# A planned kernel of four transformer layers: feature bias by small products, first layernorm of the mixing as its own steps, new costs in the planner

## The chip, the cores and the metric

The kernel runs on one core of one Trainium2 chip. A core has five engines with an instruction queue each: TensorE (PE: matrix products, with weight loads of its own, PEld), VectorE (DVE), ScalarE (ACT), GpSimd (POOL), and SyncE (SP), which issues transfers. The metric is the time on the device in microseconds (us), lower is better.

## The reference, cut to what matters

The input is one sequence of 2048 tokens with 128 features. Four layers follow one another. Each part begins with a layernorm, and its output is added to the running x:

- L0: attention with 16 heads of 64, then a mixture of 8 experts with a capacity per expert.
- L1: causal attention with 16 heads of 64, then a gated mixing of each token with the one before it.
- L2: an attention that the kernel folds into one 128x128 product, then a feed-forward of 512 with ternary weights.
- L3: attention with 16 heads, a mask by regions and a bias, then a feed-forward of 512 with binary weights.

The two parts that the change touches compute this:

```python
# the mixing (L1's feed-forward), on h = layernorm(x)
x_prev = jnp.concatenate([zeros, h[:, :-1, :]], axis=1)
xr = mu_r * h + (1.0 - mu_r) * x_prev
xk = mu_k * h + (1.0 - mu_k) * x_prev
out = sigmoid(xr @ W_r.T) * (square(relu(xk @ W_k.T)) @ W_v.T)
```

For L3's bias five small networks score each token: a hidden layer of 64 with gelu, then one sigmoid each. The five scores of a token, weighted by a softmax of `faw` per head, give one number per token and head, and this is what the kernel holds in `bias`.

## The kernel before, in words

**Tiling.** x stays in the core's memory as 16 tiles of 128 tokens (`x`), and the layernormed x as its transpose, features on partitions (`xT`, 128 x 2048). Attention runs over 8 pairs of heads, and in each pair over 8 groups of 256 query tokens. A group has 8 strips of 32 queries. A score step (L482) makes the scores of one strip and both heads: keys are cut in four quarters, and each quarter takes 32 partitions of the output, so that queries and key quarters stand on partitions and 512 keys (fewer under the causal mask) on columns. DVE scans each bank for its lowest value while it copies it out of PSUM (L492). The lowest values are turned, reduced and spread (L544, L552, L560, L567). ACT exponentiates (L594). DVE transposes 32x32 blocks (L611). PE weighs the values (L626). The head sums are added and inverted (L645, L657), the output is projected (L671), scaled (L681) and added to x by POOL (L699).

**The order of the work.** It isn't written out by hand. Every piece is a `Step` with a key (a tick, a place and its number), an engine, a cost in us, the steps that it waits for, and the buffers that it takes and uses. `run()` (L119) is a list scheduler: it walks through modelled time, and for each engine takes the step that can start first by key, with `HOP` (0.15) from engine to engine; buffers come free when the users of an older holder have ended. Steps are issued to the engines in this order, and on the chip each engine works its queue off in order, waiting where its input isn't there. The costs only set the order: they are numbers in the code, such as `max(0.25, 0.0019 * n)` for a score step of n columns with 0.1 on top for causal and 0.07 for masked ones (L500), and `0.06 + 0.00436 * self.width(4 * j)` for a transpose (L613).

**Buffers.** `Ring` and `Held` (L78, L86) hand out rotating buffers: `MISC` (three PSUM banks for all small products), `BANKS` (four PSUM banks for scores), `MID` (four), `MIXED` (three) and `PAIRED` (two buffers of 128 x 512).

**Between L1's and L3's attention.** `rest()` (L1063) is called for five spans of tiles, (0,4), (4,4), (8,4), (12,2) and (14,2). It contains the first layernorm (`normalise`, L1089), the copy of the span's last column of xT to one of two columns of `edge` (L1091), which the next span needs as its previous token, and then the mixing: ACT scales the shifted xT (L1070) and the column from `edge` (L1072), DVE adds (L1075), PE multiplies (L1104, L1079, L1083) with relu, square and sigmoid between (L1109, L1114, L1121), DVE and POOL or DVE gate and add (L1128, L1136). Then come the folded attention of L2 (L1087, L1145) and its feed-forward (L955, L964, L977, L988), with a layernorm in front of each and one behind for L3.

`features()` (L1186) makes the bias for a chunk of 512 tokens, four times. Three products and gelus (L1194, L1199), three products to five scores (L1207) and a sigmoid (L1213) give the scores `fs`, 5 x 512. The attention needs the bias with the queries of a strip on all four quarters of the partitions, so POOL copies the scores of four strips four times over (L1221, four times a chunk), PE multiplies these 128 columns by the head weights (L1228), and DVE copies the result into `bias` (L1234). The chunks get ticks around the spans' own: chunk 0 one below span (8,4), chunk 1 one below (12,2), chunks 2 and 3 one and two above (14,2).

In the page's names, a buffer has its ring's name without its number: `t` is MISC, `s` BANKS, `e` ROWS, `mid` any of MID, MIXED and PAIRED, `big` the weights of the feed-forwards.

Of the kernel before, what the change touches and what calls it, by code (L numbers as in the profile page):

```python
# [58 lines left out]
def network(ctx: ExitStack, tc: tile.TileContext, a: dict, out: bass.AP):  # L59
# [18 lines left out]
    class Ring:  # L78


        def __init__(self, pool, name, shape, bufs, ordered=True):
            self.bufs, self.takers, self.held, self.ordered = bufs, [], [], ordered
            self.make = lambda: pool.tile(list(shape), F32, tag=name, name=name, bufs=bufs)
            rings.append(self)

    class Held:  # L86


        def __init__(self, ring):
            self.ring, self.users = ring, []  # L90
# [28 lines left out]
    def run():  # L119
# [18 lines left out]
        for _ in range(len(steps)):  # L138
# [18 lines left out]
            for h in s.takes:  # L157
                h.t = h.ring.make()
                h.ring.held.append(h)
# [74 lines left out]
    def normalise(add, t0, n, after, before=(), row=None, hurry=False):  # L234


        mv, xn, pt = Held(MEANS), Held(NORMED), Held(MISC)
# [128 lines left out]
    class Pair:  # L366
# [19 lines left out]
        def projected(self, add, c, to, which, s, takes):  # L386
            pp, b = Held(MISC), self.layer.biases[which]
# [18 lines left out]
        def valued(self, add, c):  # L406
            pv, v = Held(MISC), self.v[c]
# [13 lines left out]
    class Group:  # L421
# [37 lines left out]
        def score(self, add, add_scan, k):  # L459
# [40 lines left out]
            us = max(0.25, 0.0019 * n) + (0.1 if causal else 0.07 if masked else 0.0)  # L500
# [25 lines left out]
        def spread_lowest(self, add, add_later, j, found):  # L526

            low, shift, pm, pm2 = self.lows[j], self.shifts[j], Held(MISC), Held(MISC)
# [79 lines left out]
        def turn(self, add, j, h, made):  # L608
            def do():
                e = self.e(h)[:, bass.ts(j, 4), 0 : self.width(4 * j)]  # L610
                nc.vector.transpose(e, e)  # L611

            return add(DVE, 0.06 + 0.00436 * self.width(4 * j), do, made, uses=self.rows)  # L613
# [24 lines left out]
        def sum_up(self, add, made):  # L638

            ps, r = Held(MISC), Held(SHARES)  # L640
# [21 lines left out]
        def project_out(self, tick, weighed, r):  # L662

            y, pair, oT = [Held(MISC) for h in range(2)], self.pair, self.oT
# [88 lines left out]
    def output_bias(add):  # L753
        wo, pr = Held(DOUBLE), Held(MISC)
# [27 lines left out]
    def folded(add):  # L782
        q2T, av = [Held(MID) for k in range(4)], Held(MID)
        pb, pa, pt, pw = (Held(MISC) for k in range(4))
# [44 lines left out]
    moe_w = Held(DOUBLE)  # L829
# [4 lines left out]
    def experts(add, t0, after):  # L834

        r, pl, pc, pp, pb, pickT = Held(ROUTES), Held(MISC), Held(MISC), Held(MISC), Held(MISC), Held(PAIRED)
# [71 lines left out]
        for i in range(4):  # L908
            pe, parts = [Held(MISC) for half in range(2)], Held(PAIRED)
# [37 lines left out]
    def feed_forward(add, t0, n, after, full, w1T, b1, func, w2T):  # L947

        hT, made, po = [Held(MID) for f in range(NC)], [], Held(MISC)
        for f in range(0, NC, 2):  # L950
            ph = [Held(MISC) for k in range(2)]
# [43 lines left out]
    edge = keep([P, 2], "edge")  # L995
    rests = [keep([P, 1], n) for n in ("rest_r", "rest_k")]
    ternary_w = Held(DOUBLE)

    def ternary(add):
# [14 lines left out]
        for i in range(2):  # L1014
            tot, g, half, less = (keep([P, 1], f"{n}{i}") for n in ("tot", "g", "half", "less"))
            pg, low = Held(MISC), Held(MID)
# [44 lines left out]
    edges = []  # L1061

    def rest(add, t0, n, after, hurry, made):  # L1063
        m = P * n
        xr, xk, ka, r = Held(MIXED), Held(MIXED), Held(MIXED), Held(PAIRED)
        pk, pr, pv, po = (Held(MISC) for k in range(4))
        xs, own = x[:, t0 : t0 + n, :], len(edges) % 2

        def parts(to, part):
            nc.scalar.mul(to.t[:, 1:m], xT[:, bass.ds(PAD + P * t0, m - 1)], part)  # L1070
            before = edge[:, 1 - own : 2 - own] if t0 else xT[:, PAD - 1 : PAD]
# [13 lines left out]
        def attend():  # L1085
            for i in range(n):
                nc.tensor.matmul(pv2.t[:, bass.ts(i, P)], lhsT=xT[:, cols(t0 + i)], rhs=w2, start=True, stop=True)  # L1087

        done, _ = normalise(add, t0, n, after, L1_read(t0, n), hurry=hurry)  # L1089
        kept = add(  # L1090
            DVE, 0.15, lambda: nc.vector.tensor_copy(edge[:, own : own + 1], xT[:, bass.ds(PAD + P * (t0 + n) - 1, 1)]),  # L1091
            [done] + (edge_read[-1] if edge_read else []),
        )
        read, mixed = [kept], []
        for to, part, mu in ((xk, rests[1], mu_k), (xr, rests[0], mu_r)):
            s = add(ACT, 0.3 + wide(m), lambda to=to, part=part: parts(to, part), [done] + edges[-1:] + made, takes=[to])
            mixed.append(add(DVE, 0.1 + 0.00125 * m, lambda to=to, mu=mu: mix(to, mu), [s], uses=[to]))
            read += [s, mixed[-1]]
        edge_read.append(read[1::2])
        edges.append(kept)  # L1100
# [41 lines left out]
        pv2 = po  # L1142
# [17 lines left out]
    edge_read, bu_added, ob_added = [], [], [[] for c in range(4)]  # L1160

    def L1_read(t0, n):
        return L1.readers[t0 // 4]
# [7 lines left out]
    def feature_weights(add):  # L1171

        pf = Held(MISC)
# [12 lines left out]
    def features(add, c):  # L1186

        hm, made = [Held(MID) for j in range(3)], []
        fs, pf = Held(MIXED), Held(MISC)
        for j in range(3):  # L1190
            n, ph = P if j < 2 else DH, Held(MISC)
# [12 lines left out]
        def score():  # L1204
# [5 lines left out]

        add(PE, 1.85, score, made, takes=[pf, fs], uses=hm)
        scored = add(
            ACT, 2.6, lambda: nc.scalar.activation(fs.t[0:NF, :], pf.t[0:NF, :], AF.Sigmoid, bias=eb2),  # L1213
            uses=[pf, fs],
        )
        for k in range(4):
            some, pbias = Held(PAIRED), Held(MISC)

            def spread(k=k, some=some):
                strips = fs.t[0:NF, :].rearrange("p (g q) -> p g q", q=Q)[:, 4 * k : 4 * k + 4, :]  # L1220
                nc.gpsimd.tensor_copy(  # L1221
                    some.t[0:NF, :].rearrange("p (g c q) -> p g c q", c=4, q=Q),
                    strips.unsqueeze(2).to_broadcast([NF, 4, 4, Q]),
                )

            def weigh(some=some, pbias=pbias):
                for i in range(4):
                    nc.tensor.matmul(  # L1228
                        pbias.t[:, bass.ts(i, H)], lhsT=some.t[0:NF, bass.ts(i, P)], rhs=fwT, start=True, stop=True
                    )  # L1230

            def copy(k=k, pbias=pbias):
# [176 lines left out]
```

## Time and profile before

| what | value |
|---|---|
| runs shown, median of three | 3634.2 us (3632.11 to 3635.78) |
| the profiled execution's own time | 3627.2 us |
| its span, from first to last instruction | 3625.3 us |
| mean granted PE clock | 0.984 |
| busy: PE, DVE, ACT, POOL | 97%, 92%, 72%, 16% |
| scores on PE (L482, f32) | 1514.0 us |
| weighing on PE (L626) | 1302.4 us |
| scans on DVE (L492) | 1658.7 us |
| transposes on DVE (L611) | 1504.6 us |
| exponentials on ACT (L594) | 1969.3 us |

The profile is one execution. A duration in it is that of one instruction; consecutive instructions of one engine may overlap by some tens of ns, so that the time from start to start tells what one costs. A matmul that is held back while it is in the pipeline counts as busy. In the tables, "idle before" tells how long the engine rested ahead of an instruction, and the name behind the arrow what ended that rest. One product in float32 appears as two matmuls and two weight loads ("passes").

### The profile page before, as it was taken

The numbers are of one execution on the slowest core, as the hardware profiler recorded it, in microseconds if no ns is written. First come the engines' busy times: TensorE is split into PE (matmuls) and PEld (weight loads), VectorE is DVE, ScalarE is ACT, GpSimd is POOL, SyncE is SP. The second block draws the span as 40 slices with busy tenths as digits, with TensorE's granted clock in tenths as the row PEclk, the third lists the DMA queues.
The fourth block names the chain that finished last, engine by engine and source line by source line (L and its number), as shares of the span: only waits on it lengthen the run. The fifth ranks groups of instructions, "written<-read, shape, count | busy, mean of one in ns | idle before, by whom it ended". The sixth has DMA issues, their size and how long they took to land. (4 is left out here: it accounts for less than half of the span.)

```text
span 3625.3 us, 112352 instructions
## 1 busy us (share of the span) xinstructions
PE 3522.5 (97%) x46250; PEld 1798.6 (50%) x46250; DVE 3333.3 (92%) x8275; ACT 2611.1 (72%) x7940; POOL 574.6 (16%) x1172
## 2 busy tenths in 40 slices
PE   8999999999999999999999988899999999999998
PEld 3444444444444455655555645445444454444544
DVE  8999999999999979888888874699999999999995
ACT  5677777777777667788888866477776766777775
POOL 1111011101111242111111134111111111111112
PEclk9999999999999999999999998899999999999999
DMA  1000000000000000000000000000000000000000
GB/s 45 2 5 2 5 5 2 5 2 5 5 2 5 1 5 8 6 6 6 6 6 6 6 2 4 4 5 5 2 5 2 5 5 2 5 2 2 2 5 10
DMA packets 22938, 18.77 MB, mean 5 GB/s; under 512 B 3556, under 2 KB 21612, under 8 KB 22426
## 3 DMA queue, kind: packets, MB, share of 16 engines
q1 hardware_dynamic: 22362, 11.55, 1.1%
q8 instruction: 363, 5.95, 0.7%
q14 instruction: 149, 1.22, 0.1%
q0 software_dynamic: 64, 0.06, 0.0%
HBM read 10.60 MB, written 1.05 MB: 3 GB/s over the span
## 5 line engine op out<-in xcount | busy, mean ns | idle before, releaser
L594 ACT ACTIVATE e<-e,shift 128x512 f32<-128x512 f32 (+15 forms) x3072 | 1969.3, 644 | 182.0 <-DVE shift L578 174.9
L492 DVE TENSOR_SCALAR_CACHE_REDUCE e<-s 128x512 f32<-128x512 f32 (+15 forms) x3072 | 1658.7, 588 | 58.1 <-PE s L482 57.0
L482 PE MATMUL s<-kT,qT 64*32 64x512 f32 (+8 forms) x24576 | 1514.0, 534 | 25.5 <-DVE e L492 24.1
L611 DVE STREAM_TRANSPOSE e<-e 128x2048 f32<-128x2048 f32 (+10 forms) x768 | 1504.6, 1961 | 21.9 <-ACT e L594 20.7
L626 PE MATMUL o<-e,v 128*64 128x256 f32 (+1 forms) x10496 | 1302.4, 386 | 13.3 <-DVE e L611 11.9
L626 PEld LDWEIGHTS o<-e,v 128*64 128x64 f32 x10496 | 731.1, 137 | 587.6 <-issue 233.4
L482 PEld LDWEIGHTS s<-kT,qT 64*32 64x32 f32 x24576 | 429.1, 105 | 490.2 <-DVE e L492 239.0
L594 ACT ACTIVATION_READ_ACCUMULATOR e<-e,shift 128x1 f32 x3072 | 580.0, 189 | 0.0
L560 POOL COPY all_low<-all_low 8x128 f32<-8x128 f32 x384 | 108.0, 281 | 1953.3 <-DVE all_low L552 1953.3
L699 POOL TENSOR_TENSOR x<-x,part 128x256 f32<-128x256 f32 x384 | 280.7, 731 | 562.8 <-ACT part L681 547.4
L681 ACT ACTIVATE part<-t,r 128x128 f32<-128x128 f32 x768 | 218.8, 366 | 148.9 <-PE t L671 144.8
L686 ACT COPY oT<-o 128x256 f32<-128x256 f32 x192 | 70.7, 368 | 274.7 <-PE o L626 274.6
L492 DVE DVE_READ_ACCUMULATOR e<-s 128x1 f32 x3072 | 229.7, 75 | 0.0
L390 PE MATMUL t<-xT,w 128*128 128x512 f32 x384 | 204.2, 625 | 2.7 <-ACT xT L277 2.0
L482 PE MATMUL s<-beyond,eye 64*32 64x32 bf16 x2560 | 159.8, 177 | 0.0
L671 PEld LDWEIGHTS t<-w,oT 64*128 64x128 f32 x1536 | 103.9, 188 | 98.3 <-issue 67.2
L671 PE MATMUL t<-w,oT 64*128 64x128 f32 x1536 | 141.4, 299 | 2.8 <-ACT oT L686 1.5
L482 PEld LDWEIGHTS <-regions 64*32 64x32 bf16 x1024 | 74.4, 93 | 130.1 <-issue 105.3
L586 ACT COPY shift<-t 128x8 f32<-128x8 f32 x256 | 42.2, 165 | 131.0 <-PE t L567 131.0
L552 DVE TENSOR_REDUCE all_low<-t 8x32 f32<-8x128 f32 x384 | 100.7, 262 | 27.8 <-PE t L544 26.9
L482 PE MATMUL s<-picks,regions 64*32 64x8 bf16 x1024 | 122.1, 166 | 0.0
L567 PEld LDWEIGHTS t<-ident,all_low 8*128 8x128 f32 x384 | 51.2, 133 | 134.9 <-issue 75.9
(181 smaller groups left out, 1790.8 us busy)
## 6 DMA issues: line engine op xcount, KB each, us to landing
w<-in_L_wq SPq DMA_DIRECT2D x24, 64.0 KB, 1.9
w<-in_L_wk SPq DMA_DIRECT2D x24, 64.0 KB, 2.1
w<-in_L_wv SPq DMA_DIRECT2D x24, 64.0 KB, 2.0
w<-in_L_wo SPq DMA_DIRECT2D x24, 64.0 KB, 2.1
x<-in_x SPq DMA_DIRECT2D x4, 256.0 KB, 4.7
out_x<-x SPq DMA_DIRECT2D x3, 256.0 KB, 2.3
big<-in_L_wo SPq DMA_DIRECT2D x1, 512.0 KB
big<-in_moe_w SPq DMA_DIRECT2D x1, 512.0 KB
```

Of the source, the lines that this page charges most:

```text
L390: nc.tensor.matmul(pp.t, lhsT=self.w.t[:, which, :], rhs=xT[:, cols(4 * c, 4)], start=True, stop=True)
L482: nc.tensor.matmul(s[h].t[on, bass.ds(first, size)], lhsT=lhsT, rhs=rhs, start=m == 0, stop=m == len(terms) - 1,)
L492: nc.vector.tensor_scalar(self.e(h)[:, i, 0:n], s.t[:, 0:n], 1.0, None, ALU.mult, ALU.min, accum_out=self.lows[j].t[:, h, i % 4 : i % 4 + 1],)
L552: lambda: nc.vector.tensor_reduce(all_low.t, pm.t[0:NS, 0:P].rearrange("p (c q) -> p q c", q=Q), AX.X, ALU.min),
L560: lambda: nc.gpsimd.tensor_copy(all_low4.t, all_low.t.unsqueeze(1).to_broadcast([NS, 4, Q])),
L594: nc.scalar.activation(e, e, AF.Exp, bias=self.shifts[j].t[:, h, i % 4 : i % 4 + 1], scale=-1.0, accum_out=self.sums.t[:, h, i : i + 1],)
L611: nc.vector.transpose(e, e)
L626: nc.tensor.matmul(self.o.t[bass.ds(DH * h, DH), first(t) : NS, :], lhsT=self.pair.v[c].t[:, t % 4, bass.ds(DH * h, DH)], rhs=self.e(h)[:, ...
L671: nc.tensor.matmul(y[h].t[:, bass.ts(j, P)], lhsT=oT.t[half, bass.ts(j, P)], rhs=pair.w.t[half, 3, :], start=True, stop=True,)
L681: nc.scalar.mul(part.t[:, j, :], y[h].t[:, bass.ts(j, P)], r.t[:, j, h : h + 1])
L686: lambda: nc.scalar.copy(oT.t, self.o.t.rearrange("p i q -> p (i q)")),
L699: POOL, 0.74, lambda part=part: nc.gpsimd.tensor_tensor(xs, xs, part.t, ALU.add), [divided], uses=[part]
```

## The change

There are four edits. First, buffers get names of their own for the profile. Second, two costs of the planner change: a score step from 0.0019 to 0.002 per column, its causal extra from 0.1 to 0.14 and its masked extra from 0.07 to 0.05, and a transpose from 0.06 + 0.00436 per column to 0.05 + 0.0042. Third, the first layernorm of the mixing and the copy of its last column become `first_norm`, called for all spans ahead of `rest`, with the same ticks; `edge` has a column for every tile, so that the copy doesn't wait until the column of two spans ago has been read. Fourth, the feature bias: PE multiplies 128 tokens at a time by the head weights (`weigh`, 4 products instead of 16), ACT copies the 128 x 64 results (`some`), 16 products with columns of the identity hand them to the four quarters of partitions (`hand_out`), and one DVE copy puts them into `bias`.

```diff
-            us = max(0.25, 0.0019 * n) + (0.1 if causal else 0.07 if masked else 0.0)
+            us = max(0.25, 0.002 * n) + (0.14 if causal else 0.05 if masked else 0.0)
...
-            return add(DVE, 0.06 + 0.00436 * self.width(4 * j), do, made, uses=self.rows)
+            return add(DVE, 0.05 + 0.0042 * self.width(4 * j), do, made, uses=self.rows)
...
-    edge = keep([P, 2], "edge")
+    edge = keep([P, NT], "edge")
...
+    def first_norm(add, t0, n, after, hurry):
+        done, _ = normalise(add, t0, n, after, L1.readers[t0 // 4], hurry=hurry)
+        last = t0 + n - 1
+        to, some = edge[:, last : last + 1], xT[:, bass.ds(PAD + P * (t0 + n) - 1, 1)]
+        kept[t0 + n] = add(DVE, 0.15, lambda: nc.vector.tensor_copy(to, some), [done])
+        return done
...
-        done, _ = normalise(add, t0, n, after, L1_read(t0, n), hurry=hurry)
-        kept = add(
-            DVE, 0.15, lambda: nc.vector.tensor_copy(edge[:, own : own + 1], xT[:, bass.ds(PAD + P * (t0 + n) - 1, 1)]),
-            [done] + (edge_read[-1] if edge_read else []),
-        )
-        read, mixed = [kept], []
+        read, mixed = [kept[t0 + n]], []
+        needs = [done] + made + ([kept[t0]] if t0 else [])
...
+        def weigh():
+            for i in range(4):
+                nc.tensor.matmul(
+                    pbias.t[:, bass.ts(i, H)], lhsT=fs.t[0:NF, bass.ts(i, P)], rhs=fwT, start=True, stop=True
+                )
+
+        def hand_out():
+            for q in range(4):
+                for i in range(4):
+                    nc.tensor.matmul(
+                        pall.t[bass.ts(q, Q), bass.ts(i, 4 * H)],
+                        lhsT=ident[:, bass.ts(i, Q)],
+                        rhs=some.t[:, 0 : 4 * H],
+                        start=True,
+                        stop=True,
+                    )
+
+        def copy():
+            to = bias[:, bass.ts(c, 16), :].rearrange("p (t i) h -> p i t h", i=4)
+            nc.vector.tensor_copy(to, pall.t[:, 0 : 16 * H].rearrange("p (i t h) -> p i t h", i=4, h=H))
...
-            made = add(POOL, 0.6, spread, [scored], takes=[some], uses=[fs])
-            add(PE, 0.8, weigh, [made, fwT_made], takes=[pbias], uses=[some])
-            L3.biased[c].append(add(DVE, 0.16, copy, uses=[pbias]))
+        add(PE, 0.6, weigh, [scored, fwT_made], takes=[pbias, some], uses=[fs])
+        made = add(ACT, 0.25, lambda: nc.scalar.copy(some.t[:, 0 : 4 * H], pbias.t[:, 0 : 4 * H]), uses=[pbias, some])
+        add(PE, 1.2, hand_out, [made], takes=[pall], uses=[some])
+        L3.biased[c].append(add(DVE, 0.4, copy, uses=[pall]))
...
-    for t0, n in spans:
-        rest(planner(L1.left(t0, n)), t0, n, L1.outputs(t0, n) + [bu_added[t0 // 4]], n < 4, made)
+    done = {}
+    for t0, n in mix_spans:
+        done[t0] = first_norm(
+            planner(L1.left(t0, n)), t0, n, L1.outputs(t0, n) + [bu_added[t0 // 4]], n < 4
+        )
+    for t0, n in mix_spans:
+        rest(planner(L1.left(t0, n)), t0, n, done[t0], n < 4, made)
```

`mix_spans` has the five spans of `spans`.

## The prediction, made before the changed kernel was run

> **What bounds the kernel now.** I read the page's first part, a table by stretches, the waits of two layers, and the chain and timeline of the passage between the second and third attention.
>
> The page's first part. PE's 97% alone decides nothing, since a matmul held back by the instruction before it counts as busy:
>
> ```profile
> PE 3522.5 (97%) x46250; PEld 1798.6 (50%) x46250; DVE 3333.3 (92%) x8275; ACT 2611.1 (72%) x7940; POOL 574.6 (16%) x1172
> ```
>
> The table by stretches (after the length: busy time of each engine, granted PE clock, DMA). L0's attention runs until about 1230 us, L1's until 2240, L3's from 2312:
>
> ```profile
> core 0: us, PE busy (x) PEld busy (x) DVE busy (x) ACT busy (x) POOL busy (x), PEclk, DMA share, GB/s
> 140.00:600.00 460.00, 460.00 (x5482) 211.31 (x5479) 456.75 (x936) 337.88 (x974) 48.49 (x96) 1.00 0.01 4
> 600.00:1080.00 480.00, 480.00 (x5693) 218.92 (x5699) 479.96 (x987) 355.67 (x1022) 50.69 (x101) 1.00 0.01 4
> 1400.00:2000.00 600.00, 590.47 (x10920) 353.25 (x10902) 534.12 (x1788) 491.25 (x1846) 89.15 (x179) 1.00 0.02 5
> 2200.00:2250.00 50.00, 43.51 (x255) 26.31 (x254) 21.92 (x66) 31.32 (x63) 21.68 (x33) 0.90 0.02 6
> 2250.00:2300.00 50.00, 39.55 (x156) 28.16 (x155) 16.77 (x66) 19.71 (x43) 15.87 (x30) 0.71 0.00 0
> 2500.00:3400.00 900.00, 898.89 (x11289) 441.15 (x11286) 896.97 (x1921) 641.30 (x1790) 111.42 (x277) 1.00 0.01 3
> ```
>
> In L0 and L3 DVE never rests (479.96 of 480 us, 896.97 of 900). Its work there is fixed, so those stages are bound by DVE, and a new order can only lose. In L1, where the causal mask leaves narrow tiles, DVE rests 66 us of 600 and PE 9.5: PE bounds it. The two stretches of the passage fill neither. The waits agree; first L0 (140 to 1080 us), where weight loads wait for a scan to free a bank:
>
> ```profile
> PEld s L482 <- DVE e L492: 100.0, 272, 0.8
> ```
>
> then L1 (1400 to 2000 us), where the scans wait for PE as long as PE waits for them:
>
> ```profile
> DVE e L492 <- PE s L482: 24.0, 53, 1.5
> PEld s L482 <- DVE e L492: 17.3, 52, 0.8
> ```
>
> The passage is a chain of dependent layers. The chain that ended last, from 2240 to 2275 us, has the feature bias's products (L1228) in it:
>
> ```profile
> 2260.75 1.93 PE t L390 x2
> 2262.68 6.93 PE t L1228 x32
> 2269.61 1.15 PE t L1104 x2
> ```
>
> The timeline shows that L1104, which carries the chain on, had its input (L1075, mix_muk) at 2258.0 us: it stood 6.9 us behind products that no one needed yet.
>
> ```profile
> 2257.45 0.58 DVE L1075 SCALAR_TENSOR_TENSOR mid<-xT,mix_muk,mid 128x256 f32<-128x256 f32 x1 [1.66 <-ACT mid L1072]
> 2269.54 1.22 PE L1104 MATMUL t<-mid,mix_wk 128*128 128x256 f32 x2
> ```
>
> **What the Trainium skill says.** "TensorE: Matmul & The Clock Gate", section on LDWEIGHTS: a load takes as many 1.2 GHz cycles as the weights have columns, whatever the rows, so 107 ns for 128. The trace agrees: 32 passes of L1228 (128 columns of weights, 16 columns streamed) take 3.85 us at 2212.5, 120 ns each. The same page, Part 1, the HAM clock gate: PE runs at half clock after an idle window of about 3.4 us. The granted clock of 0.71 in the sparse stretch agrees, and the same 32 passes take 6.93 us there, 217 ns each. "ScalarE: Activation LUTs", section on table sets: copy stands in every set. The trace agrees: the copy at 2260.14 follows the sigmoid of 2259.55 with no load between, so the new ACT copy brings no table load of 1.28 us.
>
> **The change part by part.**
>
> *Names and layernorm.* Names add no instruction. The layernorm steps of the mixing keep tick, operations and count; only their place among steps of equal tick changes. The copy of the last column (L1091, five times, 0.11 to 0.15 us) stays, and no longer waits for the previous span's shift (L1070, L1072). Where the trace records its wait (2.2 us in all) it ended with the copy of its own xT, which stays. 0 us; if a hidden order mattered, at most those 2.2.
>
> *Feature bias, per chunk c of 512 tokens.* Removed: four POOL spreads (0.60 us each, 9.7 us in all, on an engine 16% busy), 24 of 32 passes of weigh, three of four DVE copies (0.22). Added: an ACT copy of 128x64 (between L586's 0.165 for 8 columns and L686's 0.368 for 256; I take 0.21), the hand-out of 16 products (32 passes, as float32 takes two in the trace), and one DVE copy of 256 columns instead of four of 64 (between 0.22 and L988's 0.69 for 512; I take 0.4).
>
> The hand-out loads 32 columns (27 ns by the page's rule, an estimate) and streams 64; L1194 streams 512 in 0.43 us per pass, so 64 take 54 ns. A pass is thus between 54 ns and the 120 of L1228; I take 70, since neighbouring passes share a column strip and cannot run side by side. That is 2.2 us, 4.5 at half clock (ends 1.7 to 3.8, or 3.5 to 7.7). With 8 passes of weigh (1.0 us) PE has 3.2 us per chunk instead of 3.85, so what counts is where it stands:
>
> - c=1: the 6.93 us ahead of L1104 become 8 x 0.217 = 1.7, a gain of 5.2, if the hand-out lets L1104 pass. It must wait for weigh and the ACT copy, about 0.5 us, while L1104 is ready. It is hidden by PE's idle stretches before L1104, L1083, L1087 and L262 between 2277 and 2285 (0.88, 0.49, 0.46 and 3.65: 5.5 us). If it stands ahead of L1104 the gain is 6.93 - 1.7 - 4.5 - 0.5 = 0.2; at the dear end a loss of 3.0. I take -4.
> - c=0: L1104 at 2216.3 waited 1.5 us after its input (2214.8). I take -1, ends -1.5 and +1.
> - c=2 and c=3 fall into L3's first pair, where PE's 3.9 us are covered by DVE's saturation; DVE saves 0.88 - 0.4 in each. I take -0.5 for both.
>
> New waits: the ACT copy waits for weigh, and queued behind it on ACT are the exponentials (L594), for which DVE's transposes wait. At most one weigh, 1 to 2 us a chunk; two of four chunks meet a full DVE. I take 0 and keep +3. The ring of two "mid2" buffers has one taker per chunk where it had four, which is what the mixing's r (L1079) had to follow in order: a gain already counted at c=1.
>
> *The planner's costs.* Small in the diff, wide in reach: scores and transposes have new durations in the list scheduler, so the order of all engines is laid anew. No operation changes. The times between starts in the trace show how well the numbers fit. Transposes, two lines of DVE's timeline:
>
> ```profile
> 2406.91 2.29 DVE L611 STREAM_TRANSPOSE e<-e 128x2048 f32<-128x2048 f32 x1
> 2409.13 0.64 DVE L492 TENSOR_SCALAR_CACHE_REDUCE e<-s 128x512 f32<-128x512 f32 x1
> ```
>
> 2.22 us from start to start: the old cost is 2.29, the new 2.20. Score steps of 512 columns, from the starts of their matmuls: L0 1.05 on average (0.94 where nothing held them), old 0.97, new 1.02; L3 1.09 (1.02), old 1.04, new 1.07. In L1 the sixteen widths sum to 11.0 (10.2 unheld), old 10.3, new 11.3. The new costs are nearer to the averages, the old ones in L1 nearer to what a step costs by itself. That speaks for neither sign. Value 0; ends: a gain no greater than PE's idle time from 1230 to 2312 us (21 + 34 = 55 us), a loss without such a limit.
>
> **Sum** against the profiled execution: 3627.2 - 4 - 1 - 0.5 = 3621.7 us (span 3625.3 plus 1.9 around it). The median of the runs shown lies 7.0 above that execution, so 3628.7: about 3629.
>
> **Rivals.**
>
> 1. *PE starts to stall in L1: slower, 3650.* The score cost grows by 1.05 us over 16 steps, so by 4.2 us a pair (64 steps), while PE itself needs no more; transposes are planned 0.85 us cheaper over the sixteen widths. Work for DVE and ACT is then laid against a PE slower than the real one, and PE, which takes its queue in order, comes to its weighing before the transpose is done. The trace has one such stall, at the seam where the mixing begins:
>
> ```profile
> 2132.45 3.67 PE L626 MATMUL o<-e,v 128*64 128x256 f32 x14 [5.62 <-DVE e L611]
> ```
>
> Half of it in each of eight pairs is 8 x 2.8 = 22 us; less the 5.5 gained and with the 7.0, 3651, say 3650. It decides from 13 us on (1.6 a pair). For: PE bounds L1. Against: DVE has 66 us of rest there to be early with.
>
> 2. *DVE loses its full use in L3: slower, 3648.* The plan now puts a pair of score steps nearer to DVE's pace, while the real PE needs 1.02 of 1.07. If DVE rests 1.5% of the 1248 us from 2312 to 3560 (in L1 it rests 11%), 19 us come on top: 3628.7 + 19. For: full use leaves only losses. Against: weight loads waited 50 us for scans from 2400 to 3400, so PE is ahead there.
>
> 3. *The new order packs L1 and the passage better: faster, 3612.* 30% of the 55 us of PE's idle time is 17: 3629 - 17. For: the stall just shown, and costs nearer to the averages. Against: averages include waiting.
>
> 4. *The change doesn't do what it says:* the layernorm split is inert and the hand-out stands on the chain; then the order alone remains, near 3634. It is within the forecast's own range.
>
> **How the numbers follow.** Runs of this kernel differ by 3.7 us, so 0.2% (7.3 us) is about what can be told from no change. Forecast 0.38, own range 3618 to 3640: faster 0.15, same 0.18, slower 0.05. Rival 1 0.24 (slower 0.22, same 0.02). Rival 2 0.14 (0.13, 0.01). Rival 3 0.24 (faster 0.22, same 0.02). Together: faster 0.37, same 0.23, slower 0.40. The range of 3604 to 3664 takes in the rivals and leaves out 0.1 on either side: a gain of over 30 us, which needs more than half of the idle time, and a loss of over 30.
>
> **What would show it.** Right: the feature products ahead of the mixing take 8 passes, L1104 follows its input within 3 us, DVE stays over 99% busy in L0 and L3, L1's length from first to last score changes by less than 7 us. Wrong: hand-out passes over 120 ns; longer stalls of PE behind transposes in L1; DVE's idle time in L3 over 10 us; an L1 shorter by over 10 us.

## The result and the profile after

| | before | changed |
|---|---|---|
| median of 14 runs each | 3631.6 us (3629.5 to 3635.8) | 3635.8 us (3632.7 to 3651.9) |
| ratio with its 95% interval | 1 | 1.0020 [1.0012, 1.0029] |
| the profiled execution, and its span | 3627.2, 3625.3 us | 3634.4, 3632.4 us |
| mean granted PE clock | 0.984 | 0.984 |

The ratio says 7.3 us slower (4.4 to 10.5), the two medians alone 4.2, the two profiled executions 7.2. A second set of runs of the changed kernel, among the experiments, gave 1.0017 [1.0010, 1.0024]. Four of the changed kernel's runs took 3642.9 to 3651.9 us, at a mean granted clock of 0.979 to 0.983 where its other ten had 0.984 to 0.986, and lift the ratio above the medians. So the change costs some 4 to 7 us, 0.1 to 0.2%, no more than the 0.2% that the prediction gave as what can be told, though its interval leaves out no change at all. The forecast was a gain of 5.5 us: its sign was wrong. Its own chances were nearly even (faster 0.37, same 0.23, slower 0.40), and the median of 3635.8 us lies within the range that it gave for itself, 3618 to 3640.

In the changed kernel the lines have moved: L1075 is now L1083 (the mixing's add), L1104 is L1106 (its product), L1087 is L1095 (the folded attention's product, while L1087 is now the mixing's second product), L955 is L956, L977 is L978, and L1213, the sigmoid of the features, is L1234. New are L1213 (`weigh`), L1237 (ACT's copy), L1220 (`hand_out`) and L1230 (the copy into `bias`). Buffers have names of their own (`pk`, `xk`, `pall`).

The page's first part, changed kernel:

```profile
PE 3524.6 (97%) x46282; PEld 1788.7 (49%) x46282; DVE 3329.3 (92%) x8263; ACT 2622.3 (72%) x7950; POOL 566.8 (16%) x1156
```

The counts are those of the edit: PE +32 passes (8 + 32 in place of 32, in four chunks), DVE -12, ACT +4 copies and six more loads of an activation table (32 for 26, 1.28 us each, none of them at the new copy), POOL -16. Three of the six are at the exponentials (L594, 13 for 10), two at the feed-forward (L965, 5 for 3) and one at the gelus (L1199, 6 for 5): in the new order on ACT, functions of different tables follow one another more often. The table by stretches of the changed kernel, in the same stretches and columns as before:

```profile
core 0: us, PE busy (x) PEld busy (x) DVE busy (x) ACT busy (x) POOL busy (x), PEclk, DMA share, GB/s
140.00:600.00 460.00, 459.99 (x5478) 211.01 (x5480) 456.25 (x935) 337.38 (x971) 48.63 (x96) 1.00 0.01 4
600.00:1080.00 480.00, 480.00 (x5682) 217.59 (x5672) 479.92 (x981) 355.53 (x1023) 50.66 (x100) 1.00 0.01 3
1400.00:2000.00 600.00, 589.23 (x10865) 352.26 (x10848) 529.13 (x1777) 492.31 (x1840) 89.31 (x179) 0.99 0.02 5
2200.00:2250.00 50.00, 41.01 (x276) 24.34 (x272) 18.45 (x51) 29.65 (x63) 15.05 (x22) 0.90 0.01 3
2250.00:2300.00 50.00, 37.87 (x175) 22.61 (x175) 18.38 (x76) 22.55 (x47) 17.46 (x32) 0.80 0.01 4
2500.00:3400.00 900.00, 898.70 (x11241) 442.51 (x11237) 894.49 (x1908) 638.30 (x1782) 113.34 (x279) 1.00 0.01 3
```

L0 is as full as it was. In L1 DVE did 5.0 us less in the same 600 us (529.13 for 534.12), and in L3 2.5 us less in 900 (894.49 for 896.97): both layers have slowed a little. The stretches of the passage are still sparse.

What DVE and PE wait for in L1 (1400 to 2050 us; total us, times, longest), changed kernel:

```profile
DVE e L492 <- PE s L482: 36.5, 47, 1.4
PEld s L482 <- DVE e L492: 21.2, 66, 0.8
```

Before, these two stood at 24.0 and 17.3 over the same 650 us, which the prediction's text called 1400 to 2000 (from 1400 to 2000 the first is 22.5 before and 34.0 after). Scans wait 12 us longer for PE, fewer times. In L3 (2500 to 3400 us) one small wait has grown. Before:

```profile
DVE e L611 <- ACT e L594: 1.7, 5, 0.3
```

and in the changed kernel:

```profile
DVE e L611 <- ACT e L594: 4.2, 12, 0.3
```

That is the 2.5 us: a transpose now reaches DVE's head before ACT has made its exponentials about twice a pair of heads, where it did so once.

The passage. The chain that ended last, changed kernel:

```profile
2271.18 0.88 ACT xn L251 x2
2272.08 1.28 ACT L1234
2273.37 0.69 ACT fs L1234
2274.10 1.06 PE pbias L1213 x8
2275.16 2.00 PE pp L390 x2
2277.17 1.89 PE pall L1220 x32
2279.05 0.63 PE pk L1106 x2
```

and its timeline, the mixing's add and product with the hand-out between:

```profile
2271.00 0.48 DVE L1083 SCALAR_TENSOR_TENSOR xk<-xT,mix_muk,xk 128x256 f32<-128x256 f32 x1 [1.40 <-ACT xk L1080]
...
2277.09 1.96 PE L1220 MATMUL pall<-some,ident 128*32 128x64 f32 x32
2278.98 0.70 PE L1106 MATMUL pk<-xk,mix_wk 128*128 128x256 f32 x2
```

L1106 had its input at 2271.5 and began at 2279.0. Before, it had it at 2258.0 and began at 2269.5. The product waits 7.5 us instead of 11.5 us, but both its input and itself come later, by 13.5 and 9.5 us. What stands ahead of it is now the sigmoid with its table load on ACT (L1234), the 8 passes that wait for it (L1213), a projection of L3 (L390) and the hand-out (L1220), which did not let it pass.

To find where the time went, the start of every 128th scan (L492; 3072 in all, 128 to a pair of heads) was set against the scan of the same number in the profile of before ("7 pairs done" is the first scan of the eighth pair):

| us later than before at | L0, 7 pairs done | L1, 2 pairs done | L1, 7 pairs done | L3, 1 pair done | L3, 7 pairs done | end of span |
|---|---|---|---|---|---|---|
| changed | 2.1 | 3.4 | 6.9 | 2.5 | 5.7 | 7.1 |

The changed kernel stands 3.4 us later at L1's third pair, which by itself tells little (see below the last table). It loses 3.5 us over the next five pairs, gains 4.4 up to the end of L3's first pair, and loses 4.6 in the rest of L3 and its end. The 4.4 us are not those of the passage: L1's last pair, up to its last score, takes 3.4 us less (133.2 for 136.6), the passage from there to L3's first scan takes 1.0 more (131.9 for 130.9), and L3's first pair 1.9 less (156.1 for 158.0). So the passage as a whole did not give the gain that was predicted of it.

### The profile page after: what moved, and what is told of

The parts are those of the page before. It is cut to its first block, busy times and chain, and to the rows that moved or that the text cites. A ratio compares the mean times of both kernels' runs of the same rounds, so it can differ in the third digit from the quotient of the medians.

```text
span 3632.4 us, 112345 instructions
## 1 busy us (share of the span) xinstructions
PE 3524.6 (97%) x46282; PEld 1788.7 (49%) x46282; DVE 3329.3 (92%) x8263; ACT 2622.3 (72%) x7950; POOL 566.8 (16%) x1156
## 5 line engine op out<-in xcount | busy, mean ns | idle before, releaser
L594 ACT ACTIVATE e<-e,shift 128x512 f32<-128x512 f32 (+15 forms) x3072 | 1969.7, 645 | 198.4 <-DVE shift L578 191.6
L492 DVE TENSOR_SCALAR_CACHE_REDUCE e<-s 128x512 f32<-128x512 f32 (+15 forms) x3072 | 1658.4, 587 | 63.4 <-PE s L482 62.5
L594 ACT ACTIVATION_READ_ACCUMULATOR e<-e,shift 128x1 f32 x3072 | 581.4, 189 | 0.0
L681 ACT ACTIVATE part<-y,r 128x128 f32<-128x128 f32 x768 | 219.2, 368 | 149.5 <-PE y L671 142.4
L492 DVE DVE_READ_ACCUMULATOR e<-s 128x1 f32 x3072 | 228.3, 74 | 0.0
L390 PE MATMUL pp<-xT,w 128*128 128x512 f32 x384 | 210.4, 639 | 3.7 <-ACT part L681 3.0
L671 PEld LDWEIGHTS y<-w,oT 64*128 64x128 f32 x1536 | 106.5, 186 | 89.9 <-issue 60.4
L671 PE MATMUL y<-w,oT 64*128 64x128 f32 x1536 | 143.7, 298 | 1.3 <-ACT shift L586 0.7
L586 ACT COPY shift<-pm 128x8 f32<-128x8 f32 x256 | 42.3, 165 | 126.7 <-PE pm L567 126.7
L567 PEld LDWEIGHTS pm<-ident,all_low 8*128 8x128 f32 x384 | 51.2, 133 | 147.5 <-issue 85.8
L482 PEld LDWEIGHTS <-eye 64*32 64x32 bf16 x2560 | 98.6, 94 | 37.6 <-issue 15.6
```

The source lines that it names most:

```text
L390: nc.tensor.matmul(pp.t, lhsT=self.w.t[:, which, :], rhs=xT[:, cols(4 * c, 4)], start=True, stop=True)
L482: nc.tensor.matmul(s[h].t[on, bass.ds(first, size)], lhsT=lhsT, rhs=rhs, start=m == 0, stop=m == len(terms) - 1,)
L492: nc.vector.tensor_scalar(self.e(h)[:, i, 0:n], s.t[:, 0:n], 1.0, None, ALU.mult, ALU.min, accum_out=self.lows[j].t[:, h, i % 4 : i % 4 + 1],)
L567: lambda: nc.tensor.transpose(pm2.t[:, 0:NS], all_low4.t.rearrange("p c q -> p (c q)"), ident[0:NS, 0:NS]),
L594: nc.scalar.activation(e, e, AF.Exp, bias=self.shifts[j].t[:, h, i % 4 : i % 4 + 1], scale=-1.0, accum_out=self.sums.t[:, h, i : i + 1],)
L671: nc.tensor.matmul(y[h].t[:, bass.ts(j, P)], lhsT=oT.t[half, bass.ts(j, P)], rhs=pair.w.t[half, 3, :], start=True, stop=True,)
```

## The experiments

The experiments ran in three sets, each on one chip beside the kernel before, with at least 41 runs of it. "Old costs" and "new costs" are those of the diff: the score step's and the transpose's. The theories in play at first: the loss comes from the planner's costs (the order laid anew), from the feature products standing ahead of the mixing, or from both.

### The parts, one by one

e1_old_costs is the changed kernel with the two costs of before:

```diff
-            us = max(0.25, 0.002 * n) + (0.14 if causal else 0.05 if masked else 0.0)
+            us = max(0.25, 0.0019 * n) + (0.1 if causal else 0.07 if masked else 0.0)
...
-            return add(DVE, 0.05 + 0.0042 * self.width(4 * j), do, made, uses=self.rows)
+            return add(DVE, 0.06 + 0.00436 * self.width(4 * j), do, made, uses=self.rows)
```

> The changed kernel with the score and transpose costs of before put back; feature bias and layernorm stay as changed. Theory A (the new costs lay a worse order, the feature bias saves 4 to 5 us in the passage between L1 and L3): 0.9987 of before, 4 to 6 us faster. Theory B (the new costs are neutral, the feature bias or its ACT copy loses): as slow as the changed kernel, 1.001 to 1.002. Also under A: DVE's idle time in L3 falls back to that of before.

Measured: 0.9998 [0.9990, 1.0007]. The feature bias and the layernorm steps together are worth -0.7 us (-3.6 to +2.5), not -5.5.

e2_new_costs_only is the kernel before with the new costs and nothing else (the same lines, the other way round).

> The kernel before with nothing but the two new costs. Theory A: 1.0025, 7 to 11 us slower than before, the loss spread over L0, the seam to L1, L1 and L3. Theory B: within 0.05% of before.

Measured: 1.0007 [1.0000, 1.0014], +2.5 us (0 to 5). The costs alone hurt a little. -0.7 and +2.5 make 1.8, and together they measured 6 to 7. With intervals of 2.5 to 3 us to a side that is only just more than a sum can give; the next two runs show it more clearly.

e3_new_score_cost and e4_new_turn_cost are the changed kernel with one cost new and the other old:

```diff
e3: -            return add(DVE, 0.05 + 0.0042 * self.width(4 * j), do, made, uses=self.rows)
e3: +            return add(DVE, 0.06 + 0.00436 * self.width(4 * j), do, made, uses=self.rows)
e4: -            us = max(0.25, 0.002 * n) + (0.14 if causal else 0.05 if masked else 0.0)
e4: +            us = max(0.25, 0.0019 * n) + (0.1 if causal else 0.07 if masked else 0.0)
```

> The changed kernel with the new score cost but the transpose cost of before. If the dearer scores are what hurts (A1): 1.001 to 1.002 of before, as the changed kernel. If the cheaper transposes hurt (A2): 0.9985 to 0.9995. Under B: 1.001 to 1.002.

> The changed kernel with the new transpose cost but the score costs of before. A1 (scores hurt): 0.9985 to 0.9995. A2 (transposes hurt): 1.001 to 1.002. Under B: 1.001 to 1.002.

Measured: 0.9994 [0.9986, 1.0003] and 0.9993 [0.9986, 0.9999]. With either cost new by itself the changed kernel is no slower than before, with both it is 0.2% slower. If the two costs added up, both together would be some 4 us faster than before (-2.2 and -2.5 us, less the -0.7 that both contain). So neither of the two costs is to blame by itself; it takes both.

The profiles divide the loss further. The new transpose cost brings DVE's longer wait for exponentials in L3, with the score cost as it was. e4, the waits of DVE from 2500 to 3400 us:

```profile
DVE e L611 <- ACT e L594: 3.5, 10, 0.4
```

e1, with neither, has the 1.7 us of before. In time that is 0.5 us a pair (the last table of this section). The loss of 3.5 us over five pairs of L1 shows only where both are new: e2 has it too, e3 loses 0.9 there, and e4 and e1 nothing. The scans' wait for PE in L1 (1400 to 2050 us) goes with it: 36.5 us in the changed kernel, 35.8 in e2, 30.7 in e3, 24.0 in e4, 23.7 in e1 and 24.0 before.

### Does it repeat, and does the place of the features decide?

e6_changed_again is the changed kernel once more, unchanged, beside three that move one chunk of the feature bias.

> The changed kernel once more, beside the others on one chip. If the two edits simply add up, 1.0005 (old costs 0.9998, costs alone 1.0007): 1 to 3 us slower than before. If they work against each other, 1.001 to 1.0025, 4 to 8 us slower, and the passage between L1 and L3 is longer than with the new costs alone.

Measured: 1.0017 [1.0010, 1.0024]. Its profile follows that of the first within 0.8 us at all the marks of the table.

e7_changed_chunk1_late moves the whole of chunk 1 (hidden products, gelus, sigmoid, `weigh`, `hand_out`, copy) from ahead of the mixing's span (12,2) to behind the span (14,2):

```diff
-        features(planner((L1.left(8, 4) - 1, L1.left(12, 2) - 1, L1.left(14, 2) + 1, L1.left(14, 2) + 2)[c]), c)
+        features(planner((L1.left(8, 4) - 1, L1.left(14, 2) + 0.5, L1.left(14, 2) + 1, L1.left(14, 2) + 2)[c]), c)
```

e8_before_chunk1_late is the same edit in the kernel before; e9_old_costs_chunk1_late is the same edit in the changed kernel with both old costs.

> The changed kernel with one edit: the whole feature chain of chunk 1 gets a tick behind the mixing of the last span instead of one ahead of the mixing of (12,2). Theory P (what stands ahead of L1104 on PE, and the gelus and sigmoid ahead of the mixing on ACT, hold the passage): 4 to 9 us faster than the changed kernel, L1106 starts within 3 us of its input. Theory Q (the passage is bound by its own chain, place doesn't matter): within 2 us of the changed kernel.

> The kernel before with the same one edit of chunk 1's tick. Theory P: 5 to 10 us faster than before (0.9973 to 0.9986), since 6.9 us of products leave the chain and the mixing's input no longer stands behind chunk 1's gelus. Theory Q: within 2 us of before.

> The changed kernel with the old costs and chunk 1's feature chain late. Theory P: 5 to 10 us faster than the same without the late tick (which was 0.9998): 0.997 to 0.9985 of before, with L3 as long as before. Theory Q: 0.9995 to 1.0000.

Measured: e7 0.9995 [0.9987, 1.0003], 8 us below e6; e8 0.9982 [0.9973, 0.9991], 5.6 us (medians) below before; e9 0.9982 [0.9975, 0.9989]. The timeline of e7 at the same place:

```profile
2252.56 0.55 DVE L1083 SCALAR_TENSOR_TENSOR xk<-xT,mix_muk,xk 128x256 f32<-128x256 f32 x1 [0.57 <-ACT xk L1080]
2253.17 1.22 PE L1106 MATMUL pk<-xk,mix_wk 128*128 128x256 f32 x2 [1.77 <-DVE xk L1083]
```

The product follows its input at once, and stands 26 us earlier than in the changed kernel. So the features did stand in the mixing's way, in both kernels, and the gain that the prediction sought was there. But it takes moving the whole chain, not making its last product smaller. Part of it is given back: in e7 L3's first scan comes 12.9 us earlier than in e6 (2305.4 for 2318.3), and L3's first pair, in which three hand-outs now fall where two did, takes 5.4 us longer (161.4 for 156.0). In e8, 9.1 of 9.7 us are given back so in its profile. And e8 and e9 are equal: with chunk 1 out of the way and the costs as they were, the old and the new way of making the bias differ by nothing that these runs can tell (each interval is 0.07 to 0.09% to a side).

### The hand-out alone

e10_changed_hand1_late leaves chunk 1 where it is, and puts only its hand-out and copy behind the mixing:

```diff
+        if c == 1:
+            add = planner(L1.left(14, 2) + 0.5)
         add(PE, 1.2, hand_out, [made], takes=[pall], uses=[some])
```

> The changed kernel with only the hand-out of chunk 1 and its copy given a tick behind the last mixing: on PE, L1106 of (12,2) then comes straight behind weigh, and the hand-out behind it; the rest of the order stays. If the prediction's step is right that the hand-out's place is worth 4 us: 1.0008 of before. If what held L1106 is the chain ahead of weigh (gelus, table loads and sigmoid on ACT, for which weigh waits): no more than the 2.0 us of the hand-out itself, 1.0012 to 1.002.

Measured: 1.0015 [1.0009, 1.0022], the same as e6 within its interval. The timeline of e10:

```profile
2272.43 0.48 DVE L1083 SCALAR_TENSOR_TENSOR xk<-xT,mix_muk,xk 128x256 f32<-128x256 f32 x1 [1.40 <-ACT xk L1080]
...
2275.52 1.06 PE L1213 MATMUL pbias<-fwT,fs 5*128 5x16 f32 x8 [0.78 <-ACT fs L1234]
...
2280.01 0.60 PE L1106 MATMUL pk<-xk,mix_wk 128*128 128x256 f32 x2
2280.54 1.39 PE L1220 MATMUL pall<-some,ident 128*32 128x64 f32 x32
```

Now the hand-out does let the mixing pass, as the forecast assumed, and the product still starts 7.1 us after its input. `weigh` stands before it and waits for the sigmoid, and PE takes its queue in order; behind that are the projection L390 (2.08 us) and, where the hand-out stood, 1.80 us of L411. So the forecast's own assumption is granted, the planner fills the place with other work, and there is no gain that can be measured.

### Costs and place together

e11_new_score_chunk1_late is e7 with the old transpose cost. e12_old_costs_chunks01_late is e9 with chunk 0 moved too, behind the span (12,2):

```diff
-        features(planner((L1.left(8, 4) - 1, L1.left(14, 2) + 0.5, L1.left(14, 2) + 1, L1.left(14, 2) + 2)[c]), c)
+        features(planner((L1.left(12, 2) + 0.5, L1.left(14, 2) + 0.5, L1.left(14, 2) + 1, L1.left(14, 2) + 2)[c]), c)
```

e13_unheld_costs_chunk1_late is e7 with costs fitted to the times from start to start in the trace where nothing held the instruction:

```diff
-            us = max(0.25, 0.002 * n) + (0.14 if causal else 0.05 if masked else 0.0)
+            us = (0.19 if causal else 0.155 if masked else 0.07) + 0.0017 * n
...
-            return add(DVE, 0.05 + 0.0042 * self.width(4 * j), do, made, uses=self.rows)
+            return add(DVE, 0.097 + 0.00416 * self.width(4 * j), do, made, uses=self.rows)
```

> The changed kernel with chunk 1 late, the new score cost, and the transpose cost of before. If each new cost hurts only beside the other, or through the transposes in L3: 0.9975 to 0.9985 of before, as with both old costs. If the score cost hurts by itself: 0.9990 to 0.9995, as with both new costs.

> The changed kernel with the old costs and the feature chains of chunks 0 and 1 both behind a mixing (chunk 0 behind that of (12,2), chunk 1 behind that of (14,2)). If features ahead of the mixing are what costs in the passage: another 2 to 5 us on top of 0.9982, 0.9970 to 0.9978. If chunk 0 is now too late for L3's first group: 0.9985 or more.

> The changed kernel with chunk 1 late and costs fitted to the times from start to start of steps that nothing held (score 0.0017 per column plus 0.07, 0.155 or 0.19; transpose 0.097 + 0.00416 per column). If a better fit makes a better order: at or below 0.9975. If the fit within some per cent doesn't matter: 0.9982 within 0.0007 either way.

Measured: e11 0.9952 [0.9939, 0.9964], median 3613.5 us of five runs, 16.6 below before and 22 below the changed kernel: it is faster than both. e13 0.9954 [0.9941, 0.9968], 3614.6 us, also of five runs. e12 0.9985 [0.9978, 0.9991]: moving chunk 0 as well adds nothing to e9. e11 is faster than either of its expectations. e13 falls under its first one, that a better fit makes a better order; but e11 is as fast without the fit, so the fit is not shown to be the cause. The same move of chunk 1 is thus worth 4.4 us from e1 to e9, 8.1 from e6 to e7 and 15.2 from e3 to e11 (medians; the first and last pair are from different sets), by the costs that it meets.

Two things in the traces go with the gain of e11 and e13 over e9. The first is the stall at the seam that the prediction quoted, PE waiting for a transpose before it weighs. e9, the waits of PE from 2060 to 2190 us:

```profile
PE o L626 <- DVE e L611: 5.6, 1, 5.6
```

It is there, 5.6 us long, in all six profiles with the old score cost (before, e1, e4, e8, e9, e12), and in the eight with another (changed, e2, e3, e6, e7, e10, e11, e13) no such wait is longer than 1.0 us. The pair in which it lies, from its first scan to L1's last score, takes 136.6 to 139.4 us in five of the six (134.6 in e4) and 132.0 to 134.4 in the eight.

The second is the place of the mixing of the span (12,2). In e11 its product comes ahead of the folded attention's product of the span (8,4):

```profile
2232.81 0.70 PE L1106 MATMUL pk<-xk,mix_wk 128*128 128x256 f32 x2
...
2239.04 1.16 PE L1095 MATMUL po<-w,xT 128*128 128x128 f32 x8 [0.68 <-ACT xT L277]
```

So it does in e13 (2230.9 and 2235.7). In e9 it comes behind, 23 us later. The chain of e9:

```profile
2235.46 3.67 PE o L626 x14
2239.13 2.00 PE pv L411 x8
2241.13 0.65 PE y L671 x8
2241.77 5.12 PE o L626 x48
...
2248.20 1.17 PE po L1095 x8
...
2255.36 1.19 PE pk L1106 x2
```

and in e7 it comes behind as well (2253.2 behind 2246.1). From L1's last score to L3's first scan e11 takes 114.9 us and e13 113.0, e9 119.0 and e7 119.7. That these two make the gain of e11 over e9 (10.9 us by the ratios) fits in size, with 4.6 to 7.4 us from the first and 4.1 from the second, but it was only argued: no run took one of them away by itself.

The chain of e9 shows a third thing, which goes with the new way of making the bias. 48 passes of weighing, 5.12 us, are laid ahead of a product that a chain of layers waits for. Before, they stood behind it:

```profile
2234.77 1.16 PE L1087 MATMUL t<-w,xT 128*128 128x128 f32 x8
...
2235.85 5.19 PE L626 MATMUL o<-e,v 128*64 128x256 f32 x48
```

They stand ahead in every kernel with the new way but e12 (the changed kernel has them in three groups of 16, 1.88, 1.88 and 1.67 us on its chain), and behind in before, e2, e8 and e12.

### All of it by place

The table of the result, for all that were profiled (single profiles; us later than before):

| | L0, 7 pairs done | L1, 2 pairs done | L1, 7 pairs done | L3, 1 pair done | L3, 7 pairs done | end of span | table loads |
|---|---|---|---|---|---|---|---|
| changed | 2.1 | 3.4 | 6.9 | 2.5 | 5.7 | 7.1 | 32 |
| e6, changed again | 2.4 | 4.2 | 7.7 | 2.9 | 6.1 | 7.5 | 32 |
| e10, hand-out 1 late | 3.7 | 4.9 | 8.5 | 2.0 | 5.2 | 7.3 | 32 |
| e2, new costs only | 2.5 | 4.5 | 8.0 | -0.4 | 2.8 | 4.3 | 30 |
| e1, old costs | 5.2 | 5.5 | 5.4 | 6.0 | 6.0 | 8.0 | 28 |
| e3, new score cost | 3.1 | 2.3 | 3.2 | -0.6 | 0.0 | 1.6 | 27 |
| e4, new transpose cost | 4.1 | 3.5 | 3.4 | -3.6 | -0.8 | -1.7 | 32 |
| e7, chunk 1 late | 1.8 | 3.6 | 7.1 | -4.7 | -1.4 | -0.1 | 35 |
| e8, before, chunk 1 late | -1.0 | 2.8 | 2.7 | -0.6 | -2.2 | -0.6 | 30 |
| e9, old costs, chunk 1 late | 3.1 | 4.6 | 4.5 | 0.5 | 0.4 | 0.5 | 31 |
| e12, old costs, chunks 0 and 1 late | 4.3 | 4.4 | 4.4 | 0.1 | 0.1 | 0.2 | 30 |
| e11, new score cost, chunk 1 late | 3.1 | 1.2 | 2.2 | -14.7 | -14.1 | -12.3 | 29 |
| e13, unheld costs, chunk 1 late | 1.1 | -0.9 | 0.0 | -16.3 | -15.8 | -15.8 | 29 |

The profiled execution of before (3627.2 us) lies 4.4 us below the median of its runs, so a kernel of equal time may well stand some 4 us later here. How much single executions differ shows in e1, e8, e9 and e12: until about 2200 us they give every engine the same instructions in the same order as before, and at L1's last score they still stand 8.1, 4.0, 7.2 and 7.1 us behind it. So the first column needn't be a loss of the change. e1's profile is 5.2 us behind at the first scan of L0's second pair, long before any of its features run. What can be read with more trust are the differences within a row; over five pairs of L1 these four differ from before by 0.1 us at most.

The step from the third column to the fourth takes in more than the passage. Here it is divided, for some of the kernels (us; the folded attention's product is that of the span (8,4), L1087 before and L1095 in the changed kernel):

| | L1's last pair, first scan to last score | to the folded attention's product | to L3's first scan | L3's first pair |
|---|---|---|---|---|
| before | 136.6 | 52.2 | 78.7 | 158.0 |
| e2, new costs only | 132.7 | 52.8 | 73.2 | 158.4 |
| e1, old costs | 139.4 | 58.4 | 72.6 | 155.8 |
| changed | 133.2 | 60.4 | 71.5 | 156.1 |
| e7, chunk 1 late | 132.7 | 60.4 | 59.3 | 161.4 |
| e8, before, chunk 1 late | 137.9 | 54.1 | 63.1 | 167.1 |
| e9, old costs, chunk 1 late | 139.4 | 58.4 | 60.7 | 163.0 |
| e11, new score cost, chunk 1 late | 132.0 | 58.9 | 56.0 | 161.7 |

- Over five pairs of L1 (second to third column) the five kernels with both new costs lose 3.5 or 3.6 us (changed, e2, e6, e7, e10), e3, e11 and e13 0.9 or 1.0, the others nothing.
- Over six pairs of L3 (fourth to fifth) all with the new transpose cost lose 2.8 to 3.3 us, all others 0.6 at most, and e8 gains 1.6.
- From the third column to the fourth the new costs alone gain 8.4 us and the changed kernel 4.4; e1 loses 0.6; e9 gains 4.0, e7 11.8, e11 16.9.
- With the new way of making the bias, the folded attention's product comes 6 to 8 us later behind L1's last score (e1 against before, changed against e2), with the 48 passes laid ahead of it. What follows it is 6.1 us shorter in e1 than before, and 1.7 shorter in the changed kernel than in e2.
- The number of table loads doesn't order the times: e4 has the changed kernel's 32 at 0.9993, e7 35 at 0.9995, and e3 27 at 0.9994.

## Why the prediction was wrong, step by step

**The step that failed: "c=1 ... I take -4".** It left the mixing's input where it was, and took the products between that input and L1104 as the whole delay: the 6.93 us become 1.7, "if the hand-out lets L1104 pass". The hand-out did not; `weigh` with 8 passes and the hand-out with 32 both stood ahead. The wait still shrank by 4.0 us, from 11.5 to 7.5, as the hand-out was cheaper than reckoned. But the passage gave nothing for it: the order was laid anew ahead of the mixing too, so that its input came 13.5 us later and L1106 9.5 (L1's last score 3.4). The folded attention's product, behind which this mixing stands, came 60.4 us after L1's last score instead of 52.2, behind 48 passes of weighing; in e1, with the old costs, 58.4. What e1 gained behind that product (6.1 us) it lost ahead of it (6.2). That the 48 passes are the reason fits in size, and no run moved them alone. e1 puts the worth of the whole feature and layernorm edit at -0.7 us, e8 against e9 at nothing.

e10 shows that the hand-out's place isn't what decides: with the hand-out behind, nothing is gained. What a shorter product leaves is the chain that it waits for: a table load and gelus on ACT, six more products, a sigmoid behind a table load of its own (1.28 + 0.69 us), and PE waiting in order. e7, e8 and e9 put the worth of moving that chain at -4.4 to -8.1 us, e11 at -15.2. The prediction's "What would show it" asked for L1104 within 3 us of its input: it was 7.5 in the changed kernel, 0.1 in e7. By the prediction's own figures it could not have come: of the 11.5 us that L1104 waited, 5.2 were to go.

**The other step: "The planner's costs ... Value 0".** Alone they measured +2.5 us (0 to 5), within the ends given. Together with the features, they turned -0.7 into +6. So of the 12.8 us between the forecast and the result, 4.8 lie in the term for the features and the other 8 in the costs and in what both do together. From L1's last score to L3's first scan, the new costs alone took 126.0 us and with the features 131.9, for 130.9 before: the features take back 5.9 us there, where the forecast saw 5 gained. In L3 the new transpose cost loses 3. To add a value for the features to one for the order was the mistake in form: each edit lays the whole order anew, and no term of one kernel's order holds in the other's.

**The sizes.** A pass of the hand-out was taken at 70 ns with ends of 54 and 120. At full clock it is 38: 32 passes in 1.23 us of weight loads in e10, below the lower end. Chunk 1's in the changed kernel took 1.96 us, 61 ns a pass, at a granted clock of 0.64; the prediction had 4.5 for it at half clock, and 3.5 at the least. The groups by form of the changed kernel (busy us, mean ns of one | idle before):

```profile
L1220 PE MATMUL pall<-some,ident 128*32 128x64 f32 x128 | 6.5, 246 | 0.0
L1213 PE MATMUL pbias<-fwT,fs 5*128 5x16 f32 x32 | 5.0, 288 | 2.8 <-ACT fs L1234 2.8
L1230 DVE COPY bias<-pall 128x256 f32<-128x256 f32 x4 | 1.6, 412 | 17.0 <-PE pall L1220 17.0
```

Four chunks of both take 11.5 us at the clock granted, where the products of L1228 took 20.1 before; ACT's copy took 0.20 us and DVE's 0.412, near what was taken (0.21 and 0.4). So the work on PE did shrink, by more than forecast, and the time did not.

**Rival 1 (PE stalls in L1, 22 us)** was of the right sign and of the wrong mechanism. No long stalls behind transposes came: the one quoted went away, and PE's waits for transposes before weighing fell from 8.8 to 2.1 us (1230 to 2312 us). What grew is the scans' wait for PE, from 24.0 to 36.5 us; it went with 3.5 us over five pairs, against 22.

**Rival 2 (DVE loses full use in L3, 19 us)** was seen, at a sixth of its size: DVE's share fell from 99.7 to 99.4% and L3 lost 3.2 us over six pairs, by waits for exponentials. All kernels with the new transpose cost show the loss, and none without it.

**Rival 3 (the order packs better, 3612 us)** is there in part in the changed kernel: the 5.6 us stall is gone, and L1's last pair is 3.4 us shorter. It was not enough there. e11 and e13, with chunk 1 out of the way and other costs than the change's, came 16.6 and 15.5 us below before, near the 17 that this rival put on the order; with the change's own two costs and chunk 1 late (e7) it is 0.9995.

**What held.** DVE was over 99% busy in L0 and L3. L1 changed in length by less than 7 us (its first scan came 4.9 us later, its last score 3.4: 2186.0 for 2182.6). ACT's copy brought no table load; the six new ones are of the order. For the layernorm steps the value of 0 wasn't measured by themselves: laid out alone, they leave the order of all five engines as it was, but for one 128x1 copy that moves up two places on DVE; e1 and e9 hold them together with the features.

**Open.** Why both new costs together lose 3.5 us in L1 where the score's alone loses 1, what the 48 passes ahead of the folded attention are worth by themselves, and how the 10.9 us of e11 over e9 divide.

## What to carry to other kernels

A product that stands in front of a critical one is not the whole delay if it is itself waiting: follow its input back, on all engines, before you price what making it shorter brings, and try moving the whole chain rather than its last link. In a kernel whose order a list scheduler lays, edits don't add: each lays all queues anew, so measure the combinations, and price an edit of costs by the stalls that it can end or start, not at zero. A table of when the n-th instruction of a kind starts, against the kernel before, shows which stage gained and which lost; know first how far single profiles of the same order lie apart (here up to 8 us by the end of L1), and let the columns of such a table begin and end where a stage does.

## What the runs showed of the hardware that was not expected

At full clock, products with 32 weight columns and 64 streamed ones run at 38 ns a pass back to back, even where neighbours write the same 32 partitions of the output (32 passes in 1.23 us of loads, 1.39 us with the last stream), where the prediction reckoned at least the 54 ns of the stream at the rate of 512 columns. The trace doesn't tell by what overlap.
